# Setup copies, memsets and wide comparisons off VectorE, other buffers for the end's temporaries, and the planner's fp32 matmul length, in a post-norm decoder layer

## The chip, the cores and the metric

One core of a Trainium2 chip runs the whole layer. The metric is the device time of one execution in microseconds (us). The kernel before took 1061.91 us in the median of five runs (1059.54 to 1063.3). One more execution was profiled; it took 1060.75 us, and the instructions in its trace span 1059.0 us. "Batch" below is one of the 8 sequences of the input, counted from 0.

## The reference, cut to what matters

Every batch has 512 tokens of width 256. A layer has three parts, each ended by a layer norm:

```python
# linear attention in chunks of 32, with a decaying causal mask
S = (Qc @ Kc.T) * mask;  O = S @ Vc
x = layernorm(x + (sigmoid(x @ Wg.T) * O @ Wo.T + x))
# cross attention to ctx, 16 heads of 64
a = softmax((q_in @ Wq + bq) @ (k_in @ Wk + bk).T / 8)
x = layernorm(x + (a @ (k_in @ Wv + bv)) @ Wo + bo)
# feed-forward, 256 -> 1024 -> 256, ternary weights and a rank-16 side path
h = bitlinear(x, w_fc) + gate * (x @ v.T @ fast_b.T @ u.T)
x = layernorm(x + bitlinear(relu(h)**2, w_proj))
```

`bitlinear` replaces each weight by -1, 0 or 1 times the mean absolute value of its row. The kernel makes these ternary weights itself, once, while batch 0 runs: for `w_proj`, `neg = (w < -mean/2)` and then `tr = (w > mean/2) - neg`, both 128x1024, twice.

## The kernel before, in words

Products that need more than float16 accuracy are made of float16 pairs: every operand is split into a high half (a copy on ScalarE or GpSimd) and a low half (a subtraction, mostly on VectorE), and three matmuls stand for one (`PASSES`).

The unit of work is (batch, head pair, block of 128 queries): 8 x 8 x 4 = 256 units, in this order. A unit's `scores` are six matmuls `s` (two heads of 128x512 in PSUM); VectorE adds the mask and takes the row minimum in one instruction (`tensor_tensor_reduce`, tile `s<-s,mb`); ScalarE makes `e = exp`; `split_p` makes the high half of `ph` on ScalarE or GpSimd and the low half on VectorE; a DMA on the SP queue transposes two units' `ph` to `pT`; `attend` is 48 matmuls `av` per unit, at least four units later. Between the units stands filler: keys, queries and values for later head pairs (`gen_kv`, `gen_q`, `gen_v`: tiles `pk`, `pq`, `pvv`, `W`), the first part for the next batch (`gen_l0`), the output projection and the feed-forward of the batch before (`gen_wo`, `gen_ffn`: tiles `pwo`, `ph` in PSUM, `py`, `rh`), and in batch 0 the setup (`setup_wo`, `setup_ffn`).

Nothing of this is issued at once. The class `Recorder` records every operation (so nearly every instruction of the profile has line L451) with a priority, the index of its unit plus an offset from `LATE`. `cost` gives each operation a planned duration, `schedule` plays all engines, the buffers' slots, the DMA queue and the shared port of VectorE and GpSimd against these durations, and `emit` writes the instructions in the resulting order. On the chip each engine takes its instructions strictly in that order. `PULL` says how much filler is pulled per unit, `REACH` how far an engine but TensorE may reach past the first operation in the order of priorities, `TP` at which priorities the pieces after the last unit stand. A planned duration that is wrong therefore costs nothing by itself; it puts instructions into an order in which one may stand waiting with others behind it.

What the change touches:

- `cost` (the `PE` branch): a matmul is planned with n/2400 + 0.0025 us for n output columns, whatever its type. One matmul of the kernel is float32, `ps<-dg,ones` in `setup_ffn`, which makes the row scales `s2b`. On `POOL`, an operation of over 512 elements is planned with 0.13 + 0.9 ns each; one `is_lt` over 256 elements has an entry of its own, 0.92 us.
- `setup_decay`, `setup_small`, `setup_ffn`: one-off work for the decay mask `mdec`, the identity `identh`, the ternary weights (`fcn`/`fct` for `w_fc`, `pjn`/`pjt` for `w_proj`), and the side path (`vst`, `fbs`, `ust`).
- `attend` (its `tail` branch) and `ffn_tail`: batch 7's last two head pairs and its feed-forward, which nothing follows. Their temporaries `of`, `oh` and `y` come from the four slots of `tmp2`, and the eight `hl` of a half from the five slots of `t4`.
- after the last unit: `bf.drain()` places what is left of batch 6's feed-forward (`py6` matmuls, the product with `s2b` on VectorE into `y6`, the addition to `row6` on GpSimd), then `attend`, `wo_tail`, `ffn_tail` and `ffn_end` of batch 6 follow at the priorities of `TP`.

Of the kernel before, what the change touches and what calls it, by code (L numbers as in the profile page):

```python
# [11 lines left out]
F16 = mybir.dt.float16  # L12
# [14 lines left out]
LAG = 4  # L27
BURST = 2
MARGIN = 0.0
REACH = 9.52  # L30
SPARE = 1
DLATE = 1.6
PTS = 3
PHS = 3
NWP = 4
TP = (0.35, 0.96, 1.15, 3.0, 0.5, 5.1)
STICK = 2.09
HOLD = 0.18
HIGH = ("apaa", "paaa", "papp")
LATE = {"k": 0.0, "q": 0.0, "v": 0.53, "w": -0.33, "l": -0.41, "o": -0.91, "f": 0.31, "s": 0.0, "a": 0.91, "t": 0.0, "x": 0.31, "e": 0.0, "c": -1.28, "d": -0.95}  # L40
PULL = {"k": 5.13, "l": 2.62, "w": 3.61, "f": 4.71, "g": 5.48}

PASSES = ((0, 0), (0, 1), (1, 0))

# [109 lines left out]
class Recorder:  # L154
# [96 lines left out]
    def cost(self, o, ins, outs):  # L251

        n = max([int(np.prod(x.shape[1:])) for x in outs + ins] or [0]) if o.engine != "PE" else outs[0].idx.size
        psum = any(x.t.pool[:2] == "ps" for x in ins + outs)
        ones = sum(x.idx.size == 1 and x.t.free > 0 for x in ins)
        o.half, o.port = None, o.engine == "POOL"
        o.dma = o.method[:3] == "dma"
        if o.dma:
            x = (outs or ins)[0]
            if o.method == "dma_start_transpose":  # L260
                blocks = n / 128
                o.occ, o.lat = 0.1 * blocks + 0.4, 0.115 * blocks + 0.55
            else:
                size = {F32: 4, F16: 2}.get(x.t.dt, 1)
                o.occ, o.lat = 0.45, n * size * x.shape[0] / (380e3 if self.prio < 0 else 210e3) + (1.2 if size == 1 else 0.1)
        elif o.engine == "PE":
            o.occ = n / 2400 + 0.0025
            o.lat = o.occ + 0.17
            if ins[0].p1 - ins[0].p0 == 64:
                o.half = ins[0].p0  # L270
        elif o.engine == "DVE":
            lat = 0.145 + n * 1.042e-3
            if o.method == "tensor_tensor_reduce":
                o.occ, o.lat = 0.615, 0.8
                return
            if not psum and o.method in ("tensor_copy", "tensor_scalar") and n >= 512:
                lat = 0.12 + n * 0.62e-3
            if psum and ones and o.method == "scalar_tensor_tensor":
                lat += 0.065
            if n <= 8:  # L280
                lat = 0.19 if o.method == "reciprocal" else 0.175 if o.method == "bn_aggr" else 0.145
            o.occ, o.lat = lat - 0.085, lat
            o.port = not psum and o.method in ("tensor_tensor", "scalar_tensor_tensor", "tensor_scalar", "tensor_copy")
        elif o.engine == "ACT":
            lat = 0.165 + n * 0.83e-3 + (0.0 if psum else 0.04) + 0.07 * ones
            o.occ, o.lat = (lat + 0.01, lat + 0.12) if "accum_out" in o.kw else (lat - 0.11, lat)
        elif o.engine == "POOL":
            if o.method == "tensor_tensor":
                lat = 0.3 + n * 1.67e-3 if n <= 512 else 0.2 + n * 1.9e-3
                if o.args[3] == ALU.pow:  # L290
                    lat = 0.42 + 0.16 * n
            else:
                lat = 0.13 + n * 0.9e-3 if n > 512 else 0.92 if n == 256 and o.kw == {} and o.method == "tensor_scalar" and o.args[-1] == ALU.is_lt else 0.62 if n > 256 else 0.56 if n > 8 else 0.22 + n * 5e-3
            o.occ, o.lat = lat - 0.03, lat
# [178 lines left out]
def decoder_kernel(ctx: ExitStack, tc: tile.TileContext, ins: dict, out: bass.AP):  # L473
# [104 lines left out]
    def setup_decay(dif):  # L578
        nc.scalar.activation(ld, ld, AF.Tanh, scale=0.5)
        nc.vector.tensor_scalar(ld, ld, 1.0, 0.5, ALU.add, ALU.mult)  # L580

        sq = cst.tile([128, 4], F32, name="sq")
        pw = cst.tile([128, 32], F32, name="pw")
        fac = cst.tile([128, 32], F32, name="fac")
        for i in range(4):
            nc.scalar.activation(sq[:, i:i + 1], sq[:, i - 1:i] if i else ld, AF.Square)
        for i in range(5):
            nc.vector.scalar_tensor_tensor(fac if i else pw, dif[:, 2 * i], sq[:, i - 1:i] if i else ld, dif[:, 2 * i + 1], ALU.mult, ALU.add)
            if i:
                nc.vector.tensor_tensor(pw, pw, fac, ALU.mult)  # L590
        nc.vector.memset(mdec, 0.0)
        for g in range(4):
            r = slice(32 * g, 32 * g + 32)
            nc.vector.scalar_tensor_tensor(mdec[r, r], pw[r, :], 1.0 / WS, dif[r, 10, :], ALU.mult, ALU.mult)
# [6 lines left out]
        return ident  # L601

    def setup_small(ident):
        nc.vector.tensor_copy(identh, ident)
        for t in (bq, bk):
            nc.scalar.activation(t, t, AF.Copy, scale=WS)

# [46 lines left out]
    def setup_ffn():  # L654
# [19 lines left out]
        for i in range(2):  # L674
            st = t4(f"pjs{i}", [128, HID], F32)
            nc.sync.dma_start(st, ins["w_proj"][i * 128:(i + 1) * 128])
            th = cst.tile([128, 2], F32, name=f"thpj{i}")
            absmean(sp2[:, i:i + 1], th, st.unsqueeze(1), 1, HID, f"pj{i}")
            tr = tmp2(f"pjt{i}", [128, HID], F16)
            neg = t4(f"pjn{i}", [128, HID], F32)  # L680
            nc.vector.tensor_scalar(neg, st, th[:, 1:2], None, ALU.is_lt)
            nc.vector.scalar_tensor_tensor(tr, st, th[:, 0:1], neg, ALU.is_gt, ALU.subtract)
            nc.sync.dma_start_transpose(tpj[:, :, i * 128:(i + 1) * 128], tr)
            yield 6
# [6 lines left out]
            nc.vector.tensor_scalar(dg[:, i, :], identh, sp2[:, i:i + 1], 1.0 / 16.0, ALU.mult, ALU.mult)  # L691
        pb = misc("ps2")
        nc.tensor.matmul(pb[:, :D], ones, dg.rearrange("p a n -> p (a n)"), start=True, stop=True)
        nc.vector.tensor_copy(s2b, pb[:, :D])
        yield 6

        nc.vector.memset(vst, 0.0)
        sv = tmp2("sv", [128, 2, RANK])
        nc.sync.dma_start(sv, ins["vT"].rearrange("(c p) r -> p c r", p=128))
        split(vst[:, :, 0:RANK], vst[:, :, 96:96 + RANK], sv, WS)  # L700
        for g in (32, 64):
            nc.vector.tensor_copy(vst[:, :, g:g + RANK], vst[:, :, 0:RANK])

        gt = cst.tile([128, 1], F32, name="gt")
        nc.sync.dma_start(gt, ins["gate"].broadcast_to([128, 1]))
# [8 lines left out]
        fb = cst.tile([RANK, RANK], F32, name="fb")  # L714
        nc.sync.dma_start(fb, ins["fast_b"])
        fbs = cst.tile([RANK, 2, 128], F16, name="fbs")
        nc.vector.memset(fbs, 0.0)
        split(fbs[:, 0, 0:RANK], fbs[:, 1, 0:RANK], fb, 1.0)
        for g in (32, 64, 96):
            nc.vector.tensor_copy(fbs[:, :, g:g + RANK], fbs[:, :, 0:RANK])  # L720
        uT = t4("uT", [RANK, 2, HID], F16)
        for a in range(2):
            for n in range(2):
# [5 lines left out]
        for n in range(2):  # L729
            pu = misc(f"pz{n}")  # L730
            for i, (a, c) in enumerate(PASSES):
                nc.tensor.matmul(pu, fbs[:, a, :], uT[:, c, n * 512:(n + 1) * 512], start=(i == 0), stop=(i == 2))
            sl = slice(n * 512, (n + 1) * 512)
            nc.scalar.activation(ust[:, sl], pu, AF.Copy, scale=1.0 / WS)
            tl = tmp2(f"ul{n}", [128, 512])
            nc.vector.scalar_tensor_tensor(tl, pu, 1.0 / WS, ust[:, sl], ALU.mult, ALU.subtract)
            nc.vector.tensor_copy(ust[64:96, sl], tl[64:96])
            yield 4


# [289 lines left out]
    def ffn_tail(b, i, base, step_):  # L1030
        row = rows[b]
        rh, py = {}, {}
        ts = slice(256 * i, 256 * i + 256)
        PL = 3
        for s_ in range(8 + PL):
            nc.prio = base + step_ * s_
# [2 lines left out]
            if s_ < 8:  # L1039
                j = s_  # L1040
                r4 = ffn_h(b, j, ts, zst, f"{b}_{i}", True)
                hl = t4(f"rhl{i}{j}", [128, 2, 256])
                if i == 0 or j % 2:
                    nc.scalar.activation(r4, r4, AF.Square)
                else:
                    nc.vector.tensor_tensor(r4, r4, r4, ALU.mult)
                if j % 2:
                    nc.scalar.copy(hl[:, 0], r4)
                else:
                    nc.vector.tensor_copy(hl[:, 0], r4)  # L1050
                (nc.vector if j % 3 == 2 or (i == 1 and j == 7) else nc.gpsimd).tensor_tensor(hl[:, 1], r4, hl[:, 0], ALU.subtract)
                rh[j] = hl
# [10 lines left out]
            yield  # L1063
        for t in range(2):
            tt = 2 * i + t
            y = tmp2(f"yl{tt}", [128, D])
            nc.vector.tensor_tensor(y, py[t], s2b, ALU.mult)
            nc.vector.tensor_tensor(row[:, tt], row[:, tt], y, ALU.add)
            layernorm(b, row, EPS, "c", tt, 1, True)
# [63 lines left out]
    def attend(u):  # L1133
# [12 lines left out]
        if tail:  # L1146
            if qt == 0:
                oT[b, p] = wk.tile([128, 2, T], F16, tag="oT", name=f"oT{b}_{p}", bufs=8)
            if qt % 2:
                d = den[b, p][:, qt - 1:qt + 1, :]  # L1150
                nc.vector.reciprocal(d, d)
                of = tmp2(f"ofl{p}{qt}", [128, 2, 2, DH])
                nc.vector.scalar_tensor_tensor(of, av[b, p][:, qt - 1:qt + 1], sc, d.unsqueeze(3).broadcast_to([128, 2, 2, DH]), ALU.mult, ALU.mult)
                oh = tmp2(f"ohl{p}{qt}", [128, 2, 2, 128], F16)
                ofv = of.rearrange("p t h n -> p t (h n)")
                nc.scalar.copy(oh[:, 0], ofv)
                nc.vector.tensor_tensor(oh[:, 1], ofv, oh[:, 0], ALU.subtract)
# [89 lines left out]
    def at(i, off):  # L1247
        now[0], nc.prio = i, i + off
# [84 lines left out]
            if pend:  # L1333
                attend(pend.pop(0))

    at(U, 1)
    bf.drain()
    at(U, TP[0])
    rest(len(pend) - 4)
# [63 lines left out]
```

## Time and profile before

| | us |
|---|---|
| median of 5 runs | 1061.91 |
| the profiled execution | 1060.75 |
| its span in the trace | 1059.0 |
| TensorE busy (matmuls) | 998.6 |
| VectorE busy | 986.8 |
| ScalarE busy | 879.2 |
| GpSimd busy | 545.5 |
| mean granted TensorE clock | 0.989 |

The profile is one execution. Busy time counts an engine's own instructions; a stretch's idle time is its length less the busy time. The view of waits says for which instruction of which engine an engine sat idle. Names such as `av<-v,pT` are output and inputs of an instruction by the kernel's tile names. An instruction of VectorE or ScalarE is listed with its whole latency; the next one starts about 0.1 us before it ends, so that 0.69 us listed is 0.60 us from start to start.

### The profile page before, as it was taken

How to read it: one execution, taken by the hardware profiler on the slowest of the kernel's cores; microseconds unless marked ns; L12 is line 12 of the kernel's file. 1: busy time of each engine (PE TensorE's matmuls, PEld its weight loads, DVE VectorE, ACT ScalarE, POOL GpSimd, SP SyncE). 2: the span in 40 equal slices, each digit the busy share in tenths (PEclk: the TensorE clock that was granted, in tenths of full speed). 3: DMA queues.
4: the chain of work that ended last, by engine and by line, in shares of the span. 5: the costliest groups of instructions: out<-in, count | busy, mean ns of one | idle time of the engine just before them, and what ended most of it. 6: DMA issues, size and time to landing. Idle time of an engine off the chain costs nothing.

```text
span 1059.0 us, 29949 instructions
## 1 busy us (share of the span) xinstructions
PE 998.6 (94%) x11976; PEld 638.7 (60%) x11976; DVE 986.8 (93%) x2101; ACT 879.2 (83%) x1876; POOL 545.5 (52%) x513
## 2 busy tenths in 40 slices
PE   7986879999999999999999999999999999999986
PEld 4644545665666656665566656765567656664764
DVE  7999989999899989999899989999899998998976
ACT  7787778889987998789977898879977889878836
POOL 0252282256841597345961577426962548443635
PEclk9999989999999999999999999999999999999989
DMA  8379799999999999999999999999999999999861
GB/s 306 100 142 184 141 210 183 164 178 195 189 177 202 164 181 173 204 152 189 185 183 208 143 209 173 189 200 152 195 166 214 156 183 169 189 165 197 144 117 41
DMA packets 646636, 185.65 MB, mean 175 GB/s; under 512 B 628448, under 2 KB 641376, under 8 KB 646496
## 3 DMA queue, kind: packets, MB, share of 16 engines
q1 hardware_dynamic: 645632, 183.42, 95.8%
q8 instruction: 93, 1.52, 0.6%
q10 hardware_dynamic: 864, 0.32, 0.1%
q14 instruction: 47, 0.39, 0.1%
HBM read 21.18 MB, written 4.19 MB: 24 GB/s over the span
## 4 chain that ended last, share of the span: by engine, by line
PE 45%; DVE 17%; ACT 16%; DMA 9%; issue 5%; POOL 5%; SPq 2%; ACTq 0%; POOLq 0%; DVEq 0%
PE s L451 8%; PE av L451 8%; DMA pT<-ph 6%; DVE s L451 5%; ACT e L451 5%; PE pk L451 5%; DVE ph L451 4%; PE pq L451 4%; PE pwo L451 4%; ACT r L451 4%; PE py L451 4%; PE pvv L451 3%; ACT ph L451 3%; SPq L451 2%; DVE W L451 2%
## 5 line engine op out<-in xcount | busy, mean ns | idle before, releaser
L451 ACT ACTIVATE e<-s,nm 128x512 f32<-128x512 f32 x512 | 354.7, 706 | 99.6 <-DVE nm L451 82.2
L451 DVE SCALAR_TENSOR_TENSOR ph<-e,ph 128x1024 f16<-128x1024 f32 x256 | 330.2, 1297 | 27.6 <-ACT ph L451 25.2
L451 DVE CUSTOM_DVE_ANT_0 s<-s,mb 128x512 f32<-128x512 f32 x512 | 342.3, 710 | 5.5 <-PE s L451 4.0
L451 PEld LDWEIGHTS <-pT 128*128 128x128 f16 x6144 | 197.9, 98 | 58.0 <-issue 29.5
L451 PE MATMUL av<-v,pT 128*128 128x64 f16 x6144 | 212.1, 194 | 11.2 <-DMA pT<-ph 11.0
L451 PE MATMUL s<-W 64*128 64x512 f16 x1536 | 206.2, 379 | 12.9 <-ACT e L451 10.9
L451 POOL TENSOR_SCALAR ph<-e 128x1024 f16<-128x1024 f32 x70 | 85.7, 1225 | 227.5 <-ACT e L451 226.2
L451 ACT ACTIVATE ph<-e 128x1024 f16<-128x1024 f32 x186 | 200.1, 1081 | 2.6 <-DMA pT<-ph 0.4
L451 PEld LDWEIGHTS <-W 64*128 64x128 f16 x1536 | 64.2, 94 | 111.0 <-issue 60.1
L451 POOL TENSOR_TENSOR oh<-of,oh 128x512 f16<-128x512 f32 x62 | 86.6, 1397 | 65.0 <-ACT oh L451 63.1
L451 PEld LDWEIGHTS <-wqkv 128*128 128x128 f16 x768 | 70.3, 98 | 82.4 <-issue 18.7
L451 ACT ACTIVATION_READ_ACCUMULATOR e<-s,nm 128x1 f32 x512 | 113.9, 222 | 0.0
L451 PE MATMUL pk<-ctxh,wqkv 128*128 128x512 f16 x384 | 103.0, 382 | 6.0 <-POOL ctxh L451 5.9
L451 PE MATMUL pvv<-wqkv,ctxh 128*128 128x256 f16 x768 | 102.0, 274 | 0.3 <-DVE v L451 0.3
L451 POOL TENSOR_TENSOR rh<-r,rh 128x512 f16<-128x512 f32 x56 | 74.5, 1336 | 52.1 <-ACT rh L451 52.1
L451 PE MATMUL pq<-x1T,wqkv 128*128 128x512 f16 x384 | 97.4, 380 | 0.3 <-DVE bob L451 0.3
L451 PEld LDWEIGHTS <-ctxh 128*128 128x128 f16 x768 | 71.4, 98 | 26.0 <-issue 13.0
L451 PEld LDWEIGHTS <-oT 128*128 128x128 f16 x768 | 73.7, 99 | 20.5 <-issue 5.2
L451 PE MATMUL pwo<-wo,oT 128*128 128x256 f16 x672 | 84.2, 276 | 0.4 <-ACT e L451 0.4
L451 DVE DVE_READ_ACCUMULATOR2_ANT nm<- 128x1 f32 x512 | 72.5, 142 | 0.0
L451 PE MATMUL ph<-x2T,tfc 128*128 128x512 f16 (+1 forms) x288 | 68.9, 358 | 0.0
L451 PE MATMUL py<-tpj,rh 128*128 128x256 f16 x448 | 58.4, 273 | 0.0
(190 smaller groups left out, 1494.5 us busy)
## 6 DMA issues: line engine op xcount, KB each, us to landing
row<-in_x SPq DMA_DIRECT2D x8, 512.0 KB, 5.2
xs<-in_xT SPq DMA_DIRECT2D x7, 512.0 KB, 5.1
ctxs<-in_ctxT SPq DMA_DIRECT2D x7, 512.0 KB, 4.4
out_dram<-row SPq DMA_DIRECT2D x7, 512.0 KB, 3.6
wqs<-in_wqkv SPq DMA_DIRECT2D x6, 512.0 KB, 7.7
pT<-ph SPq DMA_TRANSPOSE x131, 7.5
wos<-in_wo SPq DMA_DIRECT2D x4, 256.0 KB, 2.7
fcs<-in_w_fc SPq DMA_DIRECT2D x2, 512.0 KB, 5.4
```

Source lines behind the costliest of these rows:

```text
L451: getattr(real[x.engine], x.method)(*[r(a) for a in x.args], **{k: r(a) for k, a in x.kw.items()})
```

## The change

The parts of the diff, those that only repeat a pattern cut:

```diff
-REACH = 9.52
+REACH = 9.66
-TP = (0.35, 0.96, 1.15, 3.0, 0.5, 5.1)
+TP = (0.0, 2.0, 0.8, 3.0, 0.5, 5.1, 2.0)
-LATE = {... "w": -0.33, ... "t": 0.0, ...}
+LATE = {... "w": -0.48, ... "t": -0.55, ...}
-PULL = {"k": 5.13, "l": 2.62, "w": 3.61, "f": 4.71, "g": 5.48}
+PULL = {"k": 4.41, "l": 2.62, "w": 3.61, "f": 4.71, "g": 4.5}
...
         elif o.engine == "PE":
-            o.occ = n / 2400 + 0.0025
+            o.occ = n / 2400 + 0.0025 if ins[0].t.dt is F16 else n / 200
...
-        nc.vector.memset(mdec, 0.0)
+        nc.gpsimd.memset(mdec, 0.0)
-        nc.vector.tensor_copy(identh, ident)
+        nc.scalar.copy(identh, ident)
...
-            nc.vector.tensor_scalar(neg, st, th[:, 1:2], None, ALU.is_lt)
+            nc.gpsimd.tensor_scalar(neg, st, th[:, 1:2], None, ALU.is_lt)
...
-        nc.vector.tensor_copy(s2b, pb[:, :D])
+        nc.scalar.copy(s2b, pb[:, :D])
-        nc.vector.memset(vst, 0.0)
+        nc.gpsimd.memset(vst, 0.0)
         for g in (32, 64):
-            nc.vector.tensor_copy(vst[:, :, g:g + RANK], vst[:, :, 0:RANK])
+            nc.scalar.copy(vst[:, :, g:g + RANK], vst[:, :, 0:RANK])
-        nc.vector.memset(fbs, 0.0)
+        nc.gpsimd.memset(fbs, 0.0)
         for g in (32, 64, 96):
-            nc.vector.tensor_copy(fbs[:, :, g:g + RANK], fbs[:, :, 0:RANK])
+            nc.scalar.copy(fbs[:, :, g:g + RANK], fbs[:, :, 0:RANK])
...
-            nc.vector.tensor_copy(ust[64:96, sl], tl[64:96])
+            nc.scalar.copy(ust[64:96, sl], tl[64:96])
...
+        rhl = wk.tile([128, 8, 2, 256], F16, tag=("pT", "ph")[i], name=f"rhl{i}", bufs=(PTS, PHS)[i])
-                hl = t4(f"rhl{i}{j}", [128, 2, 256])
+                hl = rhl[:, j]
-            y = tmp2(f"yl{tt}", [128, D])
+            y = wk.tile([128, D], F32, tag="x1T", name=f"yl{tt}", bufs=2)
...
-                of = tmp2(f"ofl{p}{qt}", [128, 2, 2, DH])
+                of = wk.tile([128, 2, 2, DH], F32, tag="x1T", name=f"ofl{p}{qt}", bufs=2)
-                oh = tmp2(f"ohl{p}{qt}", [128, 2, 2, 128], F16)
+                oh = wk.tile([128, 2, 2, 128], F16, tag="ctxh", name=f"ohl{p}{qt}", bufs=2)
...
-    at(U, 1)
+    at(U, TP[6])
     bf.drain()
```

`TP[0]` places the attends after the last unit, `TP[1]` and `TP[2]` the first half of the last feed-forward, the new `TP[6]` the rest of batch 6's. `LATE["w"]` is the offset of the setup, `LATE["t"]` that of the row minima, `PULL["k"]` the pull of keys, queries and values, `PULL["g"]` that of the feed-forward of batch 6 during batch 7. `neg` in the fifth part is `pjn`, 128x1024 float32, once for each of two halves of `w_proj`. Since the planner sees other durations and priorities, the order of nearly all instructions moves somewhat on every engine; the number of matmuls and of DMAs stays.

More of the change, by code (lines that the diff above doesn't have):

```diff
@@ L39 @@
 HIGH = ("apaa", "paaa", "papp")
-LATE = {"k": 0.0, "q": 0.0, "v": 0.53, "w": -0.33, "l": -0.41, "o": -0.91, "f": 0.31, "s": 0.0, "a": 0.91, "t": 0.0, "x": 0.31, "e": 0.0, "c": -1.28, "d": -0.95}
-PULL = {"k": 5.13, "l": 2.62, "w": 3.61, "f": 4.71, "g": 5.48}
+LATE = {"k": 0.0, "q": 0.0, "v": 0.53, "w": -0.48, "l": -0.41, "o": -0.91, "f": 0.31, "s": 0.0, "a": 0.91, "t": -0.55, "x": 0.31, "e": 0.0, "c": -1.28, "d": -0.95}
+PULL = {"k": 4.41, "l": 2.62, "w": 3.61, "f": 4.71, "g": 4.5}
 PASSES = ((0, 0), (0, 1), (1, 0))
```

## The prediction

> **What bounds the kernel now.** I read the page's slices first, for where TensorE (PE) is not full, then the busy time by stretches, then who PE waited for.
>
> ```profile
> PE   7986879999999999999999999999999999999986
> ...
> DVE  7999989999899989999899989999899998998976
> ...
> PEclk9999989999999999999999999999999999999989
> ```
>
> Each digit is 26.5 us. PE falls short in the first six slices and the last two; from there to there it is full. The stretches in us (length, then busy PE, weight loads, VectorE = DVE, ScalarE = ACT, GpSimd = POOL, granted clock) say how much:
>
> ```profile
> 53.00:160.00 107.00, 85.03 (x967) 49.05 (x962) 99.21 (x223) 81.64 (x183) 50.08 (x46) 0.95 0.91 170
> ...
> 260.00:960.00 700.00, 687.38 (x8438) 441.45 (x8436) 664.92 (x1390) 603.92 (x1270) 398.16 (x357) 1.00 1.04 182
> 960.00:1006.00 46.00, 43.47 (x529) 27.77 (x528) 39.51 (x77) 38.71 (x86) 23.64 (x19) 0.96 1.01 165
> 1006.00:1031.00 25.00, 20.55 (x306) 16.26 (x303) 18.85 (x46) 9.15 (x23) 9.30 (x11) 0.89 0.74 124
> 1031.00:1059.00 28.00, 18.84 (x158) 14.22 (x156) 17.46 (x55) 18.81 (x47) 15.96 (x27) 0.93 0.12 39
> ```
>
> In the setup stretch, 53 to 160, PE is idle for 21.97 us and DVE for 7.79: DVE is the bound there. In the middle PE is busy for 687.38 of 700, so an engine relieved there gains nothing. After the last scores (1006) PE is idle again, and a chain through all engines sets the end. What PE waited for in the setup stretch:
>
> ```profile
> PE s L451 <- ACT e L451: 7.3, 8, 1.7
> PE av L451 <- DMA pT<-ph: 4.7, 3, 1.8
> PE pk L451 <- POOL ctxh L451: 2.5, 2, 1.6
> PE ps L451 <- DVE dg L451: 2.2, 1, 2.2
> ```
>
> Scores wait for `e`, which frees their PSUM bank and itself waits for DVE's row minimum: late DVE shows as waits on ACT. The base is the profiled execution's 1060.75 us (span 1059.0 and 1.75 around it); the median of the five runs is 1.16 higher.
>
> **Setup.** DVE loses `pjn` 2 x 0.747, `ust` 2 x 0.414, `s2b` 0.425, `vst` 2 x 0.168, `fbs` 3 x 0.155: 3.55 us listed, some 2.9 from start to start. Three memsets and `identh` (0.72) go as well, but stood in DVE's first 5.7 us, 3.4 of which it sat waiting for a load: 0. With `s2b` goes DVE's wait of 0.7 for the product before it. DVE's wait of 0.8 for the row sums of the second `w_proj` half should go too: that half's load was issued at 92.87 and ended ACT's wait at 97.3; in the changed order DVE has 11 us of other work between `pjt` of the first half and these sums, against 7.5 for transpose issue, load (4.43) and sums. Moving work past the first reduction of batch 1's second head pair, which the orders set side by side show, is another 0.6. Together -5.0.
>
> ACT takes eight copies; by its nearest rows (128x256 from PSUM 0.37, 16x512 0.57, 0.2 for small ones) 2.6 us. ACT is idle for 25.4 of these 107, and `s2b`, `vst`, `ust` are first used after 239: 0; up to 2.6 if ACT were the late one. POOL's three memsets (DVE's: 0.165) run before 3 us: 0.
>
> POOL also takes `pjn`, and there lies the price. Rows for one POOL instruction on SBUF:
>
> ```profile
> L451 POOL TENSOR_SCALAR fcn<-fcs,thfc x8: 915/921/1778, 64.0 to 81.5; 128x256 f32<-128x256 f32 x8
> ```
> ```profile
> 1004.20 1.04 POOL L451 TENSOR_SCALAR ph<-e 128x1024 f16<-128x1024 f32 x1 [0.32 <-ACT e L451]
> ```
> ```profile
> 1004.29 2.03 DVE L451 SCALAR_TENSOR_TENSOR ph<-e,ph 128x1024 f16<-128x1024 f32 x1
> ```
>
> Below stands the multiplication, 1.04 for 1024 elements (the planner assumes 1.05); above, four times the comparison's 0.915: 3.66. The comparison is the same operation, so I lean there: 0.21 as a one-element POOL row takes, and four times the remaining 0.705, an estimate of 3.0. DVE's `pjt` waits for it, in order, with reductions, `ph` and (second half) `dg` queued behind. The changed order puts a `ph` (1.13) and two reductions (1.25) between the thresholds and the first `pjt`, a W (0.65), a reduction (0.65) and a reciprocal (0.1) before the second. Cover 2.4 and 1.4: stalls 0.6 and 1.6.
>
> The third line adds a second price. DVE's `ph` takes 1.21 alone; started during POOL's instruction (ends 1005.24) it takes 2.03: it stood until POOL was done. So `pjn` and the first `ph` exclude each other. If `ph` wins, `pjt` stalls 1.13 + 3.0 - 2.4 = 1.8; if `pjn` wins, DVE loses 3.0. I take 1.8 + 1.6 = 3.4, between 0 (1.04 each) and 3.66 + 2.3 = 6.0. POOL itself is free: it idles 18 us from 95 to 113. The Trainium skill says it as a rule that speaks against this move (SBUF — State Buffer, "Who interferes with whom"): of a two-input DVE instruction and a GpSimd one, whichever issues first holds the shared port pair to its end and the other fully blocks. The 2.03 agrees; by that rule with POOL first the stage's sum would be -0.4 where I put -1.6.
>
> Setup: -5.0 + 3.4 = **-1.6**, bounds -5.0 and +1.0.
>
> The float32 product: `ps` takes 1.21 on the chain, the planner allowed 0.11. PE's 2.2 us before it were a wait for `dg`, not for the product, so the true length moves only what stands behind it: 0, bounds -1 and +0.5, within the bounds above.
>
> **Middle.** The same matmuls, PE full. 12.6 us idle over six batches, in waits of 0.3 to 1.2 (`zh`, `e`, `ctxh`). The new priorities shuffle these: 0, bounds -2 and +2.
>
> **End.** Put together from matmuls' start-to-start times (256 columns 0.109, `av` 0.029), PE's work after the last scores is 33.7 us in the old order and 38.5 in the new: 50 `py` matmuls of batch 6 come after them instead of before, 6 of another product leave. So 4.8 us of PE move from a stretch where PE is nearly full to one where it idles 4.45 (1006 to 1031).
>
> From the scores of unit (7,5,0) to the last ones took 41.2 us, with PE's work 41.1; now PE needs 36.5, ACT 34.0, DVE 32.8. At the share that 960 to 1006 shows (43.47 of 46) 36.5 becomes 38.6: -2.6. Behind the last scores 4.8 less 4.45 idle leaves +0.3. DVE's product for `y62` and POOL's addition (1.43 to 2.24) now stand ahead of the third layer-norm tile of batch 7, but run while PE makes `pwl`: 0, up to +1. One thing is better: the last `ph` stood behind `ofl`, which waited from 12.7 to 15.05 for a transposed `pT`; now one of its halves stands ahead. The chain then ran through other pieces, so 0, bound -2.3.
>
> The other buffers take no wait away that the trace shows, and their slots (`pT`, `ph`, `x1T`, `ctxh`) are free by then: 0. If the last attend still held a `pT`, the first `rhl` would come up to 1 late.
>
> End: **-2.3**, bounds -4.8 and +4.8 (next). Sum -3.9: **1056.8 us**.
>
> **Rivals.**
> - *The kept work is not hidden* (slower). The stretch from (7,5,0) may be paced by DVE, ACT and the SP queue, whose transposes stand back to back from 987.3 to 1019.9, and not by PE. Then it still takes 41.2 and the 4.8 us of `py` come on top of 53.4: +4.8 - 1.6 = +3.2, **1064.0**. It decides when the tail grows by 3.7 more than the stretch shrinks. Against: PE's own sum there equals the elapsed time.
> - *POOL's comparison eats the relief* (same). Stalls of 6.0, setup +1.0, end -2.3: **1059.5**. For: the comparison's row; against: `ph` may take its turn first.
> - *The setup follows DVE all the way* (faster still). `pjn` at the multiplication's pace, no stall: -5.0; half of DVE's other idle time (6.3) goes as orders improve, -3; the end gives -4: **1049**. Against: transposes leave SP back to back from 74 to 116, so `pT` may become the next bound.
> - *It does nothing*: gains and losses of the shuffled order cancel, 1060.75; counted with the second rival.
>
> **How the numbers follow.** Forecast 0.50 (1054 to 1059), not hidden 0.18, eaten or nothing 0.17, all the way 0.15. The range leaves out half of the last and half of the slower one: 1050 to 1064. A measurement tells about 0.2% from no change, 2.1 us here. Faster: 0.15, 0.47 of the forecast and 0.04 of the eaten case: 0.66. Same: 0.16. Slower: 0.18.
>
> **What would show it.** Right: `pjn` on POOL near 3 us, DVE idle before two `pjt` about 3 us together, PE idle in 53 to 160 near 20, the last scores some 4 us earlier, and 53 to 54 us from them to the end. Wrong: `pjn` near 1 us, a `ph` of over 4 us beside it, a tail of 58 us, or PE idle time in the middle that is not 12 to 13 us.

## The result, and the profile after

The kernel after takes 1064.32 us in the median of 30 runs (1060.53 to 1066.55), the kernel before 1061.6 in 54 runs beside them (1058.65 to 1066.82). The ratio is 1.0023, with a 95% interval of 1.0016 to 1.003: slower by 2.5 us, where 1056.8 was forecast. The profiled execution took 1065.45 us, its span is 1063.7.

The slices of the page of the kernel after, each digit now 26.6 us:

```profile
PE   7977879999999999999999999999999999999996
...
DVE  7998799999899989999899998999899998999986
...
PEclk9998889999999999999999999999999999999999
```

The shape is the same. VectorE (DVE) has an 8 and a 7 in slices 4 and 5 where it had 9, TensorE (PE) does not fill up for it, and the granted clock falls to 8 in slices 4 and 5 where it was 9 (slice 6 had an 8 before as well). The same stretches as before (length, busy PE, weight loads, DVE, ScalarE = ACT, GpSimd = POOL, granted clock), the last one 5 us longer:

```profile
53.00:160.00 107.00, 82.21 (x901) 45.65 (x900) 96.89 (x212) 82.37 (x189) 50.19 (x40) 0.87 0.88 161
260.00:960.00 700.00, 683.82 (x8389) 438.35 (x8388) 658.61 (x1377) 599.07 (x1257) 397.70 (x357) 1.00 1.01 181
960.00:1006.00 46.00, 43.76 (x527) 24.86 (x525) 45.38 (x95) 44.25 (x98) 27.38 (x24) 1.00 1.09 186
1006.00:1031.00 25.00, 22.76 (x393) 19.48 (x393) 21.67 (x45) 14.10 (x34) 12.73 (x12) 1.00 1.02 165
1031.00:1064.00 33.00, 23.32 (x204) 17.87 (x201) 21.45 (x66) 20.68 (x52) 18.76 (x32) 0.94 0.10 33
```

In the setup stretch PE idles for 24.8 us (21.97 before), although DVE was relieved: DVE's own idle time rose from 7.79 to 10.11, so the relief turned into waiting. Its wait for PE's scores rose by 2.8, as much as the two waits behind POOL's comparisons (2.5) add; first before, then after:

```profile
DVE s L451 <- PE s L451: 1.1, 2, 0.9
```
```profile
DVE s L451 <- PE s L451: 3.9, 3, 2.2
```

In the middle PE idles for 16.2 (12.6 before), in the first 25 us after 1006 for 2.2 (4.45 before). The waits of PE in the setup stretch show where its time went (total, times, longest):

```profile
PE s L451 <- ACT e L451: 12.4, 8, 6.1
PE av L451 <- DMA pT<-ph: 3.0, 4, 2.0
PE pu L451 <- ACT uh L451: 2.6, 1, 2.6
PE s L451 <- DVE W L451: 1.8, 1, 1.8
PE ps L451 <- DVE dg L451: 1.8, 1, 1.8
```

Scores waited for `e` for 12.4 us instead of 7.3, and half of that is one wait. The timeline of all engines around it (start, duration, engine, tiles, and in brackets the idle time before and its releaser) lets it be followed back:

```profile
77.41 1.16 POOL L451 TENSOR_TENSOR oh<-of,oh 128x512 f16<-128x512 f32 x1
77.48 1.37 DVE L451 SCALAR_TENSOR_TENSOR fct<-fcs,thfc,fcn 128x256 f16<-128x256 f32 x1
...
81.32 2.05 DVE L451 SCALAR_TENSOR_TENSOR fct<-fcs,thfc,fcn 128x256 f16<-128x256 f32 x3
...
81.41 1.29 POOL L451 TENSOR_SCALAR ph<-e 128x1024 f16<-128x1024 f32 x1
...
81.83 1.06 ACT L451 ACTIVATE abpj<-pjs 128x1024 f16<-128x1024 f32 x1 [2.03 <-DVE fct L451]
...
83.29 1.21 DVE L451 SCALAR_TENSOR_TENSOR ph<-e,ph 128x1024 f16<-128x1024 f32 x1
...
84.60 0.69 ACT L451 ACTIVATE e<-s,nm 128x512 f32<-128x512 f32 x1 [1.61 <-DVE sp L451]
...
85.43 1.44 PE L451 MATMUL s<-W 64*128 64x512 f16 x5 [6.14 <-ACT e L451]
```

Read from below: PE waited 6.14 us for ACT's `e`. ACT sat for 2.03 us with `abpj` (the row sums of `w_proj`, setup work) at the head of its queue, because its buffer was free only after a `fct` of DVE, the first of the three at 81.32. The `e` behind it then needed a buffer that DVE's `ph` of 83.29 to 84.50 frees (the view names `sp`, a row of DVE that ends at about the same time), and this `ph` stood behind four reductions and the three `fct`. Two of the four `fct` ran long: 1.37 us beside POOL's `oh`, and the middle one of the three 1.25 us beside POOL's `ph`, where the other two take 0.48 and 0.47. No instruction of this chain is one that the change moved to another engine. They only stand in another order than before.

Around the wait PE lost more than the 6.14 us, as the granted clock shows. In short stretches the kernel after:

```profile
80.00:86.00 6.00, 0.57 (x4) 0.27 (x4) 6.00 (x15) 2.56 (x7) 2.72 (x4) 0.54 0.32 62
86.00:92.00 6.00, 6.00 (x29) 2.08 (x24) 4.57 (x7) 5.59 (x13) 3.66 (x1) 0.60 1.00 187
```

and the kernel before:

```profile
80.00:86.00 6.00, 4.20 (x82) 3.23 (x79) 6.00 (x18) 5.75 (x13) 2.45 (x3) 1.00 0.86 163
86.00:92.00 6.00, 4.65 (x46) 2.60 (x45) 6.00 (x11) 5.92 (x15) 0.00 (x0) 1.00 0.73 134
```

The clock is 0.54 in the stretch of the wait and 0.60 in the 6 us after it, where PE is fully busy; before it was 1.00 in both. With the stretches set where the clock changes, the kernel after reads, here and at a later place of the setup stretch:

```profile
77.10:80.50 3.40, 1.55 (x11) 0.42 (x8) 3.35 (x8) 2.70 (x6) 3.40 (x4) 1.00 0.22 43
80.50:90.70 10.20, 5.27 (x17) 1.27 (x17) 8.77 (x18) 7.25 (x17) 5.89 (x4) 0.50 0.58 110
152.20:155.60 3.40, 1.85 (x11) 0.46 (x8) 3.40 (x9) 2.88 (x6) 3.40 (x4) 1.00 1.26 264
155.60:162.40 6.80, 5.22 (x14) 2.03 (x14) 5.29 (x8) 3.70 (x10) 6.80 (x6) 0.50 1.14 181
```

The clock fell at 80.5, 1.2 us after PE's last matmul, and stayed at one half until 90.7, 5.3 us after the wait had ended. The Trainium skill has a rule (TensorE: Matmul & The Clock Gate, "What's actually happening"): a window of about 3.4 us without work halves the clock. This trace does not agree with it as the condition: in the 3.4 us ahead of the two falls shown PE was busy for 1.55 and 1.85 us, and the second fall has no wait of more than 1.8 us near it.

Where the time went and came back, by the start of DVE's first reduction of a unit (batch, head pair, block), in us against the profile of before. From the column e1 on they are experiments, which follow below:

| unit | before | after | e1 | e11 | e13 | e14 | e15 | e16 |
|---|---|---|---|---|---|---|---|---|
| (1,0,0) | 168.9 | +5.4 | -0.9 | +2.6 | -2.1 | +8.0 | +2.8 | 0.0 |
| (2,0,0) | 285.1 | +7.6 | -0.9 | +6.7 | -2.3 | +10.0 | +5.7 | +2.5 |
| (7,2,0) | 924.4 | +11.9 | +2.0 | +6.1 | 0.0 | +13.3 | +10.3 | +10.0 |
| last, (7,7,3) | 1007.6 | +5.9 | -1.4 | +6.0 | -4.0 | +7.5 | +6.5 | +4.0 |
| span | 1059.0 | +4.7 | -0.5 | +5.5 | -5.0 | +6.9 | +4.6 | +2.9 |

The kernel after loses 7.6 us up to batch 2 and 4.3 in the middle, and wins 7.2 back in batch 7 and the end. One profile is not exact to the microsecond: e1 and e13 have the order of before in batches 0 to 6 (e13 with a few instructions on other engines) and still differ from it by +2.9 and +2.3 between (2,0,0) and (7,2,0).

### The profile page after: what moved, and what is told of

Same layout as the page of the kernel before. It is cut to its first block, busy times and chain, and to the rows that moved or that the text cites. A ratio compares the mean times of both kernels' runs of the same rounds, so it can differ in the third digit from the quotient of the medians.

```text
span 1063.7 us, 29918 instructions
## 1 busy us (share of the span) xinstructions
PE 1000.5 (94%) x11976; PEld 637.5 (60%) x11976; DVE 985.9 (93%) x2087; ACT 883.0 (83%) x1885; POOL 560.6 (53%) x518
## 4 chain that ended last, share of the span: by engine, by line
PE 42%; DVE 20%; ACT 17%; DMA 12%; issue 5%; POOL 2%; SPq 1%; ACTq 0%; POOLq 0%; DVEq 0%
DMA pT<-ph 8%; PE av L451 8%; PE s L451 8%; PE pwo L451 6%; ACT e L451 6%; DVE s L451 5%; DVE ph L451 5%; ACT r L451 4%; PE pk L451 3%; PE pvv L451 3%; PE pq L451 3%; PE py L451 2%; ACT ph L451 2%; DVE W L451 2%; PE ph L451 2%
## 5 line engine op out<-in xcount | busy, mean ns | idle before, releaser
L451 DVE SCALAR_TENSOR_TENSOR ph<-e,ph 128x1024 f16<-128x1024 f32 x256 | 335.1, 1314 | 26.3 <-ACT ph L451 24.4
L451 POOL TENSOR_SCALAR ph<-e 128x1024 f16<-128x1024 f32 x70 | 95.4, 1364 | 230.9 <-ACT e L451 216.5
L451 POOL TENSOR_TENSOR oh<-of,oh 128x512 f16<-128x512 f32 x62 | 92.2, 1487 | 93.3 <-ACT oh L451 92.2
L451 ACT ACTIVATION_READ_ACCUMULATOR e<-s,nm 128x1 f32 x512 | 111.2, 217 | 0.0
L451 PE MATMUL pvv<-wqkv,ctxh 128*128 128x256 f16 x768 | 95.9, 273 | 0.2 <-ACT e L451 0.2
L451 POOL TENSOR_TENSOR rh<-r,rh 128x512 f16<-128x512 f32 x56 | 84.7, 1522 | 17.9 <-ACT rh L451 14.9
```

The lines of the kernel that those rows point to most:

```text
L451: getattr(real[x.engine], x.method)(*[r(a) for a in x.args], **{k: r(a) for k, a in x.kw.items()})
```

## The experiments

All of them compute the whole layer. Ratios are to runs of the kernel before on the same chip, with 95% intervals. The expectations name their theories by letters, with the meaning that each text gives them.

**The three parts apart, and the comparisons back.** At first the loss could sit in any of the parts, with the comparisons on POOL as the first suspect. e1 is the kernel before with the end part alone:

```diff
-TP = (0.35, 0.96, 1.15, 3.0, 0.5, 5.1)
+TP = (0.0, 2.0, 0.8, 3.0, 0.5, 5.1, 2.0)
-"g": 5.48
+"g": 4.5
...
-    at(U, 1)
+    at(U, TP[6])
```

and the other buffers of `rhl`, `yl`, `ofl` and `ohl`.

> The kernel before with the end's part of the change alone: TP, the pull g of batch 6's feed-forward, and the other buffers. Theory A (the trace of after shows batch 7 recovering some 8 us that setup and middle had lost, so the end's part is a gain by itself): 1053 to 1055 us against 1061.6, and 100 us or less from the scores of (7,5,0) to the end instead of 95 to 96 with fewer us before it. Rival B (the kept matmuls are added to the tail, not hidden): 1063 to 1065.

1059.22 us, ratio 0.9973 (0.996 to 0.9986): a gain of 2.9 us. e2 has the setup part alone (the three memsets and eight copies, the comparisons on POOL, the fp32 length in the plan):

```diff
-nc.vector.tensor_copy(s2b, pb[:, :D])
+nc.scalar.copy(s2b, pb[:, :D])
-nc.vector.tensor_scalar(neg, st, th[:, 1:2], None, ALU.is_lt)
+nc.gpsimd.tensor_scalar(neg, st, th[:, 1:2], None, ALU.is_lt)
...
```

> The kernel before with the setup's edits alone: eight copies on ScalarE, three memsets and the two wide comparisons on GpSimd, and the float32 matmul's true length in the plan; priorities and end as before. Theory A (the loss in setup comes from the order that the new priorities make, with scores behind the row sums of w_proj): within 2 us of 1061.6. Rival C (GpSimd's 2.8 to 3.7 us comparisons cause it): 1066 to 1068, with the granted clock in 53 to 160 us down from 0.95 to below 0.9.

1068.85, ratio 1.0073 (1.0053 to 1.0093). e3 has the four planning constants alone:

```diff
-REACH = 9.52
+REACH = 9.66
-"w": -0.33, "t": 0.0, "k": 5.13
+"w": -0.48, "t": -0.55, "k": 4.41
```

> The kernel before with REACH, LATE w, LATE t and PULL k of the change alone. Theory A (these four cost about 1.1 us per batch in the middle and most of the setup's 6 us): 1068 to 1072. Rival C (they only shuffle, the setup's edits cost): within 2 us of 1061.6 and 122 us per batch in the middle as before.

1070.49, ratio 1.0081 (1.0065 to 1.0098). So the end part gains, and each of the others by itself loses three times what the whole change loses: +7.5, +8.6 and -2.9 would make +13.2, and the change has +2.5. e4 is the kernel after with the two comparisons back on VectorE:

```diff
-nc.gpsimd.tensor_scalar(neg, st, th[:, 1:2], None, ALU.is_lt)
+nc.vector.tensor_scalar(neg, st, th[:, 1:2], None, ALU.is_lt)
```

> The changed kernel with the two wide comparisons back on VectorE. Theory A: the two stalls of 1.4 and 1.1 us and one of 0.8 for the port go, 1.5 us of VectorE work come back, so 1062 to 1064 against 1064.3. Rival C (the comparison on GpSimd is the loss): 1058 or less.

1064.14, ratio 1.0024 (1.0015 to 1.0033): no difference to the kernel after. The comparison on POOL, the price that the prediction argued about longest, does not look like what made it slower; but e4 is planned anew, so its order moved too. e9, e10 and e14 below hold the order.

**The constants one by one, and the setup without the comparisons.** e5 is the kernel before with only

```diff
-"t": 0.0
+"t": -0.55
```

> The kernel before with LATE t alone at -0.55 (row minima half a unit earlier). Theory T (row minima taken ahead of the low halves of ph, which free the three buffers of e, leave the exponentials without a buffer: the 6 us wait of TensorE near 79 us): 1066 to 1069 us against 1061.5, with a wait of TensorE for e of over 4 us in batch 0. Rival W (the setup moved earlier stands in front of the scores): 1060 to 1063, no such wait.

1087.86, ratio 1.0238 (1.0216 to 1.026). e6 with only

```diff
-"w": -0.33
+"w": -0.48
```

> The kernel before with LATE w alone at -0.48 (setup 0.15 of a unit earlier). Rival W: 1065 to 1069 us with the wait of over 4 us near 79 us. Theory T: 1060 to 1063.

1063.39, ratio 1.001 (0.9995 to 1.0025): not told from no change. e7 with only

```diff
-REACH = 9.52
+REACH = 9.66
-"k": 5.13
+"k": 4.41
```

> The kernel before with PULL k 4.41 and REACH 9.66 alone. Theory T and rival W both: 1060 to 1063 us; a third theory K (keys and queries pulled later starve batch 0): 1065 to 1069.

1081.71, ratio 1.018 (1.0156 to 1.0205). Alone, `t` costs 26 us and `k` with `REACH` 20; together with `w` they cost 8.6. They belong together: `t` without `k` and `REACH`, or these without `t`, is far worse than all of them or none. (`k` and `REACH` were not taken apart.) e8 is e2 with the comparisons on VectorE (the line that e4 edits, in e2):

```diff
-nc.gpsimd.tensor_scalar(neg, st, th[:, 1:2], None, ALU.is_lt)
+nc.vector.tensor_scalar(neg, st, th[:, 1:2], None, ALU.is_lt)
```

> The setup's edits alone again (against 1061.5), but with the two wide comparisons left on VectorE. Theory C2 (in the old priorities the loss of 7.5 us comes from the comparisons, planned with 1.05 us and taking 2.8 to 3.7): 1060 to 1063. Rival O (any edit of the setup reorders batch 0, and the old priorities fit the old edits alone): 1065 to 1069.

1067.46, ratio 1.005 (1.0033 to 1.0068). Against e2's 1.0073 the comparisons cost 2.3 us there, with intervals that overlap. The copies and memsets that only leave VectorE still come with a loss of 5.3 us, together with the fp32 length in the plan, which e8 also has.

That left the order. Every one of these edits changes durations or priorities in the plan, and so the order of nearly everything behind the first difference. The theory from here on is that this order costs and the moves are worth about nothing; its main rival, that the work on its new engines costs or gains by itself. The next kernels take the two apart.

**Moves without a new order, and a new order without moves.** In e9 every moved instruction is planned as before (on VectorE) but written to the engine that the change gives it, so that all other instructions keep the order of before on every engine:

```diff
+self.v2a, self.v2p = Engine(self, "DVE", "ACT"), Engine(self, "DVE", "POOL")
...
-nc.vector.tensor_copy(s2b, pb[:, :D])
+nc.v2a.tensor_copy(s2b, pb[:, :D])
-nc.vector.tensor_scalar(neg, st, th[:, 1:2], None, ALU.is_lt)
+nc.v2p.tensor_scalar(neg, st, th[:, 1:2], None, ALU.is_lt)
...
-getattr(real[x.engine], x.method)(
+getattr(real[x.emit or x.engine], "copy" if x.emit == "ACT" else x.method)(
```

> All of the setup's moves, comparisons too, but planned as before, so that every engine keeps the order of before and only the moved instructions change engine. Theory O (the moves themselves are cheap, the loss comes from the new order of everything else): the prediction's own terms, VectorE 2.9 us relieved against two stalls behind comparisons of 2.85 us with cover 1.2 each (3.3 us): within 1.5 us of 1061.5. Rival E (the moves to ScalarE and GpSimd cost by themselves): 1066 to 1069, as when the order moved too.

1061.92, ratio 1.0005 (0.9987 to 1.0022). e10 is the same with the comparisons left on VectorE (the `neg` line of e9 undone):

```diff
-nc.v2p.tensor_scalar(neg, st, th[:, 1:2], None, ALU.is_lt)
+nc.vector.tensor_scalar(neg, st, th[:, 1:2], None, ALU.is_lt)
```

> The same with the two wide comparisons left on VectorE. Theory O: 1059 to 1061 (1.5 us of VectorE relieved, no stall). Rival E: 1064 or more.

1060.47, ratio 0.9989 (0.9972 to 1.0006). e11 has the opposite: the kernel before with the fp32 length in the plan, and no instruction moved to another engine:

```diff
-o.occ = n / 2400 + 0.0025
+o.occ = n / 2400 + 0.0025 if ins[0].t.dt is F16 else n / 200
```

> The kernel before with the float32 matmul's true length in the plan and nothing else: no instruction changes, only the order from the second half of batch 0's setup on. Theory O (the constants of before fit its own order, and another order of the same work costs): 1064 to 1069. The prediction's own step (0, bounds -1 and +0.5): 1060.5 to 1062.

1064.77, ratio 1.0035 (1.002 to 1.005). The same instructions on the same engines, one of them planned truthfully, cost 3.7 us; the setup moved wholly, in the old order, costs 0.5 with an interval around zero. With the order held, the comparisons on POOL cost 1.7 us (e9 less e10), with intervals that overlap. The stretch from 53 to 160 of e11 shows that the clock went here too, without any moved instruction:

```profile
53.00:160.00 107.00, 88.31 (x937) 50.61 (x934) 97.50 (x220) 79.73 (x180) 48.52 (x46) 0.89 0.89 164
```

PE is busy for 3.3 us longer than before with 30 matmuls fewer, at a clock of 0.89 against 0.95. Busy time alone would have read as progress.

e9 also settles what the comparison itself does, in its tile's group and in DVE's waits:

```profile
L454 POOL TENSOR_SCALAR pjn<-pjs,thpj x2: 2841/3831/4821, 85.4 to 101.6; 128x1024 f32<-128x1024 f32 x2
```
```profile
DVE pjt L454 <- POOL pjn L454: 3.3, 2, 2.7
```

It takes 2.84 us undisturbed. The other time it started at 85.39, inside a `ph` of DVE (85.15 to 86.36) with a second `ph` right behind (to 87.58, with its usual 1.21), and took 4.82: by its length it ran its 2.84 after both of them. DVE waits 3.3 us for the two comparisons.

e12 takes the 6.14 us wait out of the kernel after: same order on every engine, but batch 0's `e` turn through four buffers instead of three and `abpj` goes to a free slot of `oT`.

```diff
+if t.name[:4] == "abpj":
+    tag = "oT_7"
+if t.name[:3] == "e0_":
+    tag = ("E_0", "E_1", "E_2", "x2T_0")[self.turn % 4]
+    self.turn += 1
```

> The changed kernel with every engine's order kept, but batch 0's exponentials in four buffers (x2T's, unused until batch 1, is the fourth) and the absolute values of w_proj in a free buffer of oT. Theory B (TensorE's 6.1 us near 79 us are a wait for a buffer: the exponentials stand behind a row sum that waits for a tmp2 slot and then wait for a buffer of e): that wait falls to 2 to 3 us and the time to 1060 to 1062 against 1064.3. Rival D (VectorE's order sets it and the next wait takes its place): 1063 to 1065.

1064.06, ratio 1.0022 (1.0007 to 1.0036): the same as the kernel after, to within some 1.5 us. PE's waits for `e` in the stretch did shrink, and the long one is gone:

```profile
PE s L457 <- ACT e L457: 8.8, 9, 2.3
```

12.4 became 8.8, 6.1 became 2.3, and the time did not follow. The wait that the trace shows most clearly was a symptom: with it gone, the next ones in the same order take most of its place (904 matmuls from 53 to 160, 901 in the kernel after, and a clock of 0.89 against 0.87).

**The best order, the changed order, and the part that does not add up.** e13 is e1 with the moves of e10 (all copies and memsets, written elsewhere but planned as before; the comparisons stay on VectorE):

```diff
+nc.v2a.tensor_copy(s2b, pb[:, :D])
+nc.v2p.memset(vst, 0.0)
...
```

> The end part together with the moved copies and memsets (the two comparisons stay on VectorE), every engine otherwise in the order that the end part alone has. Theory O (moves are worth about nothing, the order is what costs): the time of the end part alone or at most 0.2% less, ratio to before 0.995 to 0.998. Rival M (relieving VectorE in batch 0 is worth the predicted 5 us once the comparisons stay): 0.992 to 0.994.

1057.82, ratio 0.9948 (0.9931 to 0.9965), the fastest of all, 4.3 us under the 1062.15 of before beside it by the medians, 5.5 by the ratio. Against e1's 0.9973 the moves seem to gain 2.7 us; the intervals overlap by a little. e14 is the kernel after with every moved instruction, the comparisons too, written to VectorE at the place that the changed plan gives it. The other instructions keep the changed order:

```diff
+self.a2v, self.p2v = Engine(self, "ACT", "DVE"), Engine(self, "POOL", "DVE")
...
-nc.scalar.copy(s2b, pb[:, :D])
+nc.a2v.copy(s2b, pb[:, :D])
-nc.gpsimd.tensor_scalar(neg, st, th[:, 1:2], None, ALU.is_lt)
+nc.p2v.tensor_scalar(neg, st, th[:, 1:2], None, ALU.is_lt)
...
```

> The changed kernel with every moved instruction, the two comparisons too, back on VectorE, but at the place that the changed plan gives it; all other instructions of all engines keep the changed order. Theory O: the loss stays, ratio to before 1.000 to 1.006 (the work put back costs 0 to 3 us). Rival M (work put on ScalarE and GpSimd is what costs): the loss goes, ratio 0.995 to 0.998, as with the end part alone.

1067.01, ratio 1.0042 (1.0025 to 1.0059). Without any moved work the loss stays, and is rather larger (the intervals of e14 and of the kernel after overlap a little). The long wait of PE stays too:

```profile
PE s L454 <- ACT e L454: 13.4, 9, 6.3
```

The stretches of 53 to 160, first of e14, then of e13:

```profile
53.00:160.00 107.00, 79.50 (x895) 44.74 (x894) 99.56 (x221) 79.12 (x178) 41.28 (x37) 0.91 0.85 156
```
```profile
53.00:160.00 107.00, 87.50 (x1000) 51.54 (x999) 100.20 (x220) 84.15 (x192) 49.36 (x46) 0.94 0.95 173
```

895 matmuls run in the changed order, 1000 in the old one with the work moved (901 in the kernel after; 967 before and 993 in e1, both in the old order with nothing moved). DVE is busy for some 100 of 107 us in both: it is the order that decides how much of that lets PE go on.

e15 is the kernel after without the end part:

```diff
-TP = (0.0, 2.0, 0.8, 3.0, 0.5, 5.1, 2.0)
+TP = (0.35, 0.96, 1.15, 3.0, 0.5, 5.1)
-"g": 4.5
+"g": 5.48
...
```

with the end's buffers of before.

> The changed kernel without the end part: setup and the four priorities together. If the parts add up: +7.5 and +8.6 give 1078, ratio 1.015. If the two orders are a set that fits (theory I): the changed kernel less the end's -2.9 of its own, 1067 to 1068, ratio 1.004 to 1.007. If the end part is worth more in the new order than in the old one, over 1.008.

1066.55, ratio 1.0044 (1.0027 to 1.006). The end part is worth 2.2 us in this order (1.0044 to 1.0023) and 2.9 in the old one: it adds up. Setup and constants do not: 7.5 and 8.6 alone, 4.7 together.

e16 is e1 with the new constants from batch 1 on, so that batch 0 keeps its order:

```diff
-o.prio += LATE["t"]
+o.prio += LATE["t"] - (0.55 if o.prio >= 32 else 0.0)
-fr.pull(PULL["k"] + ...
+fr.pull(PULL["k"] - (0.72 if b else 0.0) + ...
-pick[0] + REACH
+pick[0] + REACH + (0.14 if pick[0] >= 32 else 0.0)
```

> The kernel before with the end part, and the new REACH, LATE t and PULL k from batch 1 on only, so that batch 0 keeps the order before. If the new priorities lose in batch 0 alone and gain in batch 7 (theory O as it stands): 1055 to 1058, ratio 0.993 to 0.996. If they only fit together with the new setup order (theory I): as slow as with the priorities alone or slower, 1060 to 1070, ratio 0.999 to 1.008.

1065.1, ratio 1.0029 (1.0013 to 1.0046): 6 us slower than e1. The hope that the constants only lose in batch 0 fell. By the table they lose 7.5 us between (2,0,0) and (7,2,0), of which 2.3 to 2.9 may be the spread of single profiles. Over all profiles with `t`, `k` and `REACH` changed together (after, e3, e4, e12, e14, e15, e16) this stretch takes 3.3 to 7.5 us more than before, over those with the old ones or `w` alone (e1, e2, e6, e8 to e11, e13) -0.6 to 3.2. There PE's wait for the transposes differs, in the waits of 260 to 960. Before:

```profile
PE av L451 <- DMA pT<-ph: 1.4, 2, 1.2
```

The kernel after, e16, and e13 with the old constants:

```profile
PE av L451 <- DMA pT<-ph: 4.6, 9, 1.2
```
```profile
PE av L451 <- DMA pT<-ph: 4.8, 11, 1.2
```
```profile
PE av L454 <- DMA pT<-ph: 2.1, 2, 1.2
```

One or two such waits with the order of before, eight to eleven with the new constants, some 3 us more in six batches: `attend` seems to come nearer to its transpose. (`t` alone, in e5, and `k` with `REACH` alone, in e7, have nine each.) Batch 7 gains from the same constants (+14.0 to +9.9 in e3, +10.3 to +6.5 in e15, both without the end part), for a reason that these runs don't single out.

## Why the prediction was wrong, by its own steps

- *What bounds.* The middle and the end were read rightly. "DVE is the bound there", said of the setup stretch, is borne out only in part: in the old order e10 takes copies and memsets off DVE and gains 1.2 us with an interval around zero, e13 2.7 over e1, and in the changed order DVE is as busy (99.56 of 107 in e14) with 895 matmuls done as with 1000 (100.20 in e13).
- *Setup, "-5.0 + 3.4 = -1.6, bounds -5.0 and +1.0".* **This step failed**, and with it the sum. Its prices hold: `pjn` was put at 3.0 and takes 2.84, or 3.69 behind a `ph`; the stalls of DVE were put at 1.8 and 1.6 and are 1.4 and 1.1; no wait for the copies on ACT shows in the views of their tiles. Of the reliefs one held in part: DVE's wait for the row sums went from 0.8 to 0.5, not to 0. In the kernel after the group and the wait read

```profile
L451 POOL TENSOR_SCALAR pjn<-pjs,thpj x2: 2844/3264/3685, 86.0 to 105.3; 128x1024 f32<-128x1024 f32 x2
```
```profile
DVE pjt L451 <- POOL pjn L451: 2.5, 2, 1.4
```

  The `ph` won its turn, as I took it: it started at 85.74 and `pjn` at 85.98. As an account of the moves alone the -1.6 is near what e9, e10, e13 and e14 show (+0.5; -1.2 and -2.7 without the comparisons; and, from the other side, -2.0; each uncertain by about 2). What it left out is the order of all the instructions that do not move. I priced that at -0.6, for a few instructions behind one reduction, and the bounds at +1.0 held only the comparison's stalls. The plan alone costs 3.7 in e11, the changed order without moves 4.5 in e14 with the end's gain in it, some 6.7 without.
- *fp32 length, "0, bounds -1 and +0.5".* Wrong for the same reason: +3.7 in the old plan (e11). The product did cost nothing, as argued; the order behind it did not stay.
- *Middle, "0, bounds -2 and +2".* Mis-sized. The profile has +4.3, of which about 3 are the nine waits for `pT`. PE idle time of 16.2 instead of 12 to 13 was named as a sign of it beforehand; the sign is weak, as e1 has 15.8 with the order of before in all but the last part of that stretch.
- *End, "-2.3".* The size is right, -2.9 in the old order (e1), -2.2 in the new one, but not by the terms that it was added up from, so it is luck as far as the mechanism goes. From the scores of (7,5,0) to the last ones the kernel after took 36.7 us instead of 41.2, more than the 2.6 forecast, but e15, without the end part, has 34.2, so that the constants made this. With the end part alone that stretch did not shrink: 44.1 in e1, 43.7 in e13. What they gain stands ahead of it, 4.1 and 4.4 us between the first reductions of (7,2,0) and (7,5,0). The 49 or 50 `py` matmuls did move behind the last scores, and from there to the end it is 52.0 in the kernel after and 53.4 in e1, where 53.4 was before and 53 to 54 was forecast.
- *The signs.* `pjn` and its stalls came as written. PE's idle time near 20 in the setup (24.8) and the last scores 4 us earlier (6.1 later) did not.
- *The rivals.* "The kept work is not hidden" named 1064.0, within 0.4 us of the result, by a mechanism that was absent: the end gained. "POOL's comparison eats the relief" put the stalls at 6.0; they are 2.5, and e14 has the loss with the comparisons on VectorE. "It does nothing" said that gains and losses of the shuffled order cancel; they did not, and no rival of mine had the shuffled order as a cost. "The setup follows DVE all the way" saw that DVE's relief needs an order that uses it; e13 is the nearest to it and gains 1 to 3 us over the end part, not 8.

**What stays open.** Which property of an order makes it good. e12 took the longest wait away for nothing; the sum of setup and constants is 11 us better than its parts, and no run tells why. That the order costs is shown (e11 and e14, with the same instructions on the same engines as before but for the end part); that a shorter wait at some one place would cure it is not.

## What to carry to other kernels

Where a planner with fixed queues writes the order, an edit has two prices: its instructions, and the new order of everything else. Measure them apart: write the instruction to its new engine while the plan stays as it is, and put the new plan's order on chip without the move. Here the moves were worth 0 to -3 us and the orders of the setup and the constants from nothing that can be told (e6) to +26, so a predicted relief of a few us needs a wide range on the slower side; and constants that come together in one change should not be taken over one at a time.

## What the runs showed of the hardware that was not expected

- A 128x1024 float32 comparison takes POOL 2.84 us where DVE needs 0.75; POOL's multiplication of the same size (float16 out) takes 1.04. Started inside a two-input DVE instruction it took 3.69 (in the kernel after it stood for about 0.9 us, until the `ph` of 85.74 to 86.95 was done) and, with two such in a row, 4.82 (e9). The Trainium skill (SBUF — State Buffer, "Who interferes with whom") says that the one that issues first holds the shared port pair to its end. The first case fits; in the second, by the lengths of both, the later `ph` of DVE went ahead of a POOL instruction that was already standing.
- TensorE's clock fell to one half after 3.4 us in which it was busy for 1.55 or 1.85 us, without an idle gap of 3.4 us, and stayed there for 10.2 and 6.8 us. In e12, with a wait of 2.3 us in place of the 6.14, it is at one half from 82.2 to 89.0. While it is, busy time is not work: 17 matmuls make 5.27 busy us from 80.5 to 90.7. The clock belongs beside every busy share (the setup stretch's mean is 0.95 before, 0.87 after, 0.89 in e11).
- Profiles of the same order differ by up to 3 us over 640 us. A stage's gain below that is not read from one profile.
